# Turning x and the attention by VectorE blocks and DMAs instead of by TensorE

## The chip, the cores and the metric

The kernel runs on one core of a Trainium2 chip. The metric is the device time of one execution in microseconds (us). A core has five engines that run side by side, each with its own queue in program order: TensorE (PE; its weight loads are listed as PEld), VectorE (DVE), ScalarE (ACT), GpSimd (POOL) and SyncE (SP, here used to issue DMAs). Sixteen DMA engines move the data. The data is 32-bit floats throughout.

## The reference

The input x has 128 samples of 128 nodes by 512 features; `adj` is a 128x128 matrix. Four layers follow each other, each with a residual and a layer norm. Cut to what is computed:

```python
x = norm(x + (adj @ x) @ W0 + bias)                              # layer 0

q, k, v = x @ Wq.T, x @ Wk.T, x @ Wv.T                           # layer 1
rel = adj.T * (q @ k.T)                                          # per sample, 128x128
rel = rel / l2norm(rel, rows)
x = norm(x + rel @ v)

h = x @ W2                                                       # layer 2
e = leaky_relu(s1[:, None] + s2[None, :]) * adj                  # s1 = h @ a1, s2 = h @ a2
att = softmax(e, axis=-1)
x = norm(x + elu(att @ h + beta * h))

a = adj @ x                                                      # layer 3
x = norm(x + max over features of relu(...))                     # x gets one value per row
```

Layer 2 is computed as `elu((att + beta I) @ x @ W2)`: beta is added on the diagonal of the attention, so one product serves both terms.

## The kernel before

The samples are worked off in 32 groups of four (`G = 4`, `NG = 32`). Every piece of work has a place in a table, given in steps; a group takes 28 steps, and the pieces of all groups are emitted in order of place, so that the layers of neighbouring groups interleave on each engine. The four large products (`y`, `m`, `v`, `z`) use a Strassen-like scheme of seven steps of eight matmuls, whose sums (`x_sums`, `z_sums`, ...) GpSimd computes.

TensorE multiplies along the partitions, so several operands have to be turned (transposed) first. Layer 1 turns x on TensorE, sixteen 128x128 turns a group, and ScalarE copies the result out of PSUM:

```python
def turn(b):                                    # layer 1, sample b of the group
    if b == 0:
        s["xT"] = work.tile([P, K, G * P], FP, tag="aT_x", name=f"xT_{g}")
    p = bank(f"p_xT_{g}_{b}")
    for k in range(K):
        pe.transpose(p[:, k * P : (k + 1) * P], x1[g][:, b, k * P : (k + 1) * P], ident)
    act.copy(s["xT"][:, :, b * P : (b + 1) * P], p.rearrange("p (k n) -> p k n", k=K))
```

The relation matrix of layer 1 is turned in another way: VectorE turns square blocks of 32, and sixteen DMAs put the blocks where they belong. Two samples are interleaved, so that a run is 256 bytes:

```python
def turn_rel():
    # ... tiles relB and relT
    for b in range(G):
        dve.transpose(
            s["relB"][:, b // 2].rearrange("p q (u j) -> p q u j", j=2)[:, :, :, b % 2],
            s["rel"][:, b, :].rearrange("p (q u) -> p q u", q=Q),
        )

def move_rel(a):                                # a = 0..3
    n = P // Q                                  # 32
    for q in range(Q):                          # Q = 4
        sync.dma_start(
            s["relT"][q * n : (q + 1) * n, :, 2 * a * n : 2 * (a + 1) * n],
            s["relB"][a * n : (a + 1) * n, :, q, :],
        )
```

Layer 2 makes the attention `e` (names as in the profile: `nm` the negative maximum, `rs` the reciprocal sum), turns it on TensorE, four turns a group, and VectorE adds beta on the way out of PSUM. `gather` then forms `zT` sample by sample:

```python
def weighted():
    pool.tensor_tensor(s["e"], s["e"], adj_b, ALU.mult)
# ... greatest (DVE), exps (ACT)
def divide(i):
    # ... dve.reciprocal(rs, ...)
    engine = pool if n == G else dve
    engine.tensor_tensor(e, e, rs[:, :, None].to_broadcast([P, n, P]), ALU.mult)

def turn_att(i):
    # ...
        pe.transpose(s["p"][:, b * P : (b + 1) * P], s["e"][:, b, :], ident)

def with_beta(i):
    # ...
    dve.tensor_tensor(s["eT"][...], s["p"]..., beta_b[...], ALU.add)

def gather(b):
    # ...
        pe.matmul(p[:, k * P : (k + 1) * P], x2[g][:, b, k * P : (k + 1) * P],
                  s["eT"][:, b, :], start=True, stop=True)
    act.copy(s["zT"][:, :, b * P : (b + 1) * P], ...)
```

In the profile `p_xT` are the turns of x, `p_eT` those of the attention, `p_z` the gather, `p_o` the product with relT, `p_a` layer 3, `p_y` the aggregation of layer 0, `p_rel` the scores, `p_s` the spread of s2, and `r_y`, `r_m`, `r_v`, `r_z` the steps of the four large products. The three tiles tT (the M product), v and c (the z product) rotate through three buffers of one tag, `nat`; the weights wq, wk, wv lie in them at the start.

Of the kernel before, what the change touches and what calls it, by code (L numbers as in the profile page):

```python
# [8 lines left out]
FP = mybir.dt.float32  # L9
AF = mybir.ActivationFunctionType  # L10
ALU = mybir.AluOpType
# [18 lines left out]
def kernel(  # L30
# [33 lines left out]
    pe, dve, act, pool = (InOrder(tc, e) for e in (nc.tensor, nc.vector, nc.scalar, nc.gpsimd))  # L64
    sync = InOrder(tc, nc.sync)
    B, N, D = x.shape
    P = 128
    assert N == P and D % P == 0
    K = D // P
    Q = P // 32  # L70
    H = D // 2
    G = 4
# [5 lines left out]
    work = ctx.enter_context(tc.tile_pool(name="work", bufs=1))  # L78
# [3 lines left out]
    def bank(name):  # L82
        return psum.tile([P, D], FP, tag="ps", name=name)
# [8 lines left out]
    x1, x2, x3 = {}, {}, {}  # L92
# [12 lines left out]
    bias_sb = const.tile([P, D], FP)  # L105
    nc.scalar.dma_start(bias_sb, on_all(bias0, D))

    wq_sb = work.tile([P, K, D], FP, tag="nat", name="wq_sb", bufs=3)
    nc.sync.dma_start(wq_sb, wq.rearrange("(k p) f -> p k f", p=P))
    wk_sb = work.tile([P, K, D], FP, tag="nat", name="wk_sb", bufs=3)  # L110
    nc.sync.dma_start(wk_sb, wk.rearrange("(k p) f -> p k f", p=P))
    wv_sb = work.tile([P, K, D], FP, tag="nat", name="wv_sb", bufs=3)
    nc.sync.dma_start(wv_sb, wv.rearrange("(k p) f -> p k f", p=P))

    w2_sb = const.tile([P, K, D], FP)
# [25 lines left out]
    beta_b = beta_i[:, None, :].to_broadcast([P, G, P])  # L141
# [78 lines left out]
    def emit(at, f, *args):  # L220
        pieces.append((at, lambda: f(*args)))

    def each(at, f):
        for b in range(len(at)):
            emit(at[b], f, b)

    def row(at, step, n=G):
        return [at + i * step for i in range(n)]
# [2 lines left out]
    TABLE = dict(  # L231
        load=[-20], y=row(0.5, 1), bias=row(1.3, 1), y_sums=row(5.2, 0.5), y_w=row(7, 1, 7),
        stats0=row(14.4, 0.4), norm0=[16.2], apply0=row(16.8, 0.33),
        turn=row(21.4, 1), x_sums=row(25.3, 0.5), m=row(28, 1, 7), scores=row(36.5, 1),
        masked=[39.95], squares=[40.4], turn_rel=[40.3],
        move_rel=row(41.2, 0.1), inverse=[42.5], v=row(42, 1, 7), attend=row(50.6, 1),
        residual=row(51.0, 1), dots=row(54.2, 1.1), norm1=[55.2], scale=[58.8],
        apply1=row(65.4, 0.33),
        spread=[61.6], leaky=[62.0], weighted=[63.4], greatest=[64.3], exps=[64.4],
        divide=[65.8], turn_att=[68.6], with_beta=[69.0], gather=row(71.5, 1),  # L240
        z_sums=row(75.3, 0.5), z_w=row(77, 1, 7), exp=[87.5, 88.5, 90.4, 92.0],
        elu=[87.8, 89.4, 92.8, 93.8], norm2=[95.0], apply2=row(95.7, 0.33),
        widen=[98.7, 100.0, 103.6, 104.6], top=[99.1, 100.4, 104.0, 105.0],
        stats3=[99.8, 101.1, 104.7, 105.7], norm3=[106.2], apply3=row(107, 0.33), store=[108.5],
    )

    FIRST = {1: dict(y=row(-9.5, 0.3), bias=row(-9.2, 0.3))}

    LAST = {
        NG - 3: dict(  # L250
            exp=[0.8, 1.5, 2.2, 11.0], elu=[9.7, 12.3, 14.6, 17.2], norm2=[19.5],
# [2 lines left out]
        ),  # L254
        NG - 2: dict(
            scale=[5.6], apply1=row(24.3, 0.8), spread=[6.9], leaky=[7.4], weighted=[9.0],
            greatest=[10.5], exps=[11.2], divide=[13.6], turn_att=[18.3], with_beta=[18.9],
            gather=row(36.7, 0.9), z_sums=row(39.95, 1.3),
            z_w=[40.0, 41.8, 43.5, 45.2, 47.0, 49.4, 51.1], exp=[51.5, 52.2, 56.2, 58.6],
            elu=row(56.9, 2.3), norm2=[66.1], apply2=row(67.7, 0.8), widen=row(73.0, 0.86),  # L260
# [4 lines left out]
            m=[0.0, 1.73, 3.46, 5.2, 7.4, 9.1, 10.8], scores=row(12.7, 0.9), masked=[16.4],  # L265
# [3 lines left out]
            greatest=[52.4], exps=row(53.2, 0.6), divide=row(53.9, 0.6),  # L269
            turn_att=row(54.4, 0.6), with_beta=row(54.9, 0.6), gather=[55.2, 56.1, 60.5, 65.0],  # L270
            z_w=[57.0, 61.5, 66.0, 69.5], exp=[60.6, 65.0, 69.6, 73.2],
# [10 lines left out]
    def times(g):  # L282
        t = {key: [28.0 * g + v for v in at] for key, at in TABLE.items()}
        t.update({key: [28.0 * g + v for v in at] for key, at in FIRST.get(g, {}).items()})
        t.update({key: [LAST_M + v / SLOT for v in at] for key, at in LAST.get(g, {}).items()})
# [7 lines left out]
    def left_factors(at, s, aT, tag, name, keep):  # L293

        def blk(nh, kh):
            return s[aT][:, 2 * kh : 2 * kh + 2, 2 * P * nh : 2 * P * (nh + 1)]

        def first():  # L300
            sums = work.tile([P, 3 + keep, 2, 2 * P], FP, tag=tag, name=f"s_{name}")
            s1, s2, s4 = (sums[:, i] for i in range(3))
            s3 = sums[:, 3] if keep else blk(1, 0)
            s["f"] = {1: blk(0, 0), 2: blk(0, 1), 3: s4, 4: blk(1, 1), 5: s1, 6: s2, 7: s3}
            pool.tensor_tensor(s1, blk(1, 0), blk(1, 1), ALU.add)

        emit(at[0], first)
        emit(at[1], lambda: pool.tensor_tensor(s["f"][6], s["f"][5], blk(0, 0), ALU.subtract))
        emit(at[2], lambda: pool.tensor_tensor(s["f"][7], blk(0, 0), blk(1, 0), ALU.subtract))
        emit(at[3], lambda: pool.tensor_tensor(s["f"][3], blk(0, 1), s["f"][6], ALU.subtract))  # L310
# [129 lines left out]
    def layer1(g, t):  # L440
        s = {}

        def turn(b):
            if b == 0:
                s["xT"] = work.tile([P, K, G * P], FP, tag="aT_x", name=f"xT_{g}")
            p = bank(f"p_xT_{g}_{b}")
            for k in range(K):
                pe.transpose(
                    p[:, k * P : (k + 1) * P], x1[g][:, b, k * P : (k + 1) * P], ident
                )  # L450
            act.copy(
                s["xT"][:, :, b * P : (b + 1) * P], p.rearrange("p (k n) -> p k n", k=K)
            )

        def begin_middle():
            s["tT"] = work.tile([P, K, G * P], FP, tag="nat", name=f"tT_{g}", bufs=3)

        def middle_block(nh, ch):
            return s["tT"][:, 2 * ch : 2 * ch + 2, 2 * P * nh : 2 * P * (nh + 1)]
# [48 lines left out]
            pool.tensor_tensor(s["rn"], s["n2"], mhalf, ALU.pow)  # L508

        def begin_values():  # L510
            s["v"] = work.tile([P, G, D], FP, tag="nat", name=f"v_{g}", bufs=3)

        def attend(b):
            s["o", b] = bank(f"p_o1_{g}_{b}")
# [37 lines left out]
        def scale_dots():  # L552
# [11 lines left out]
            )  # L564
            s12[g] = s["d"]

        each(t["turn"], turn)
        left_factors(t["x_sums"], s, "xT", "s_x", f"x_{g}", 1)
        product(t["m"], f"m_{g}", by_columns, s, "m", middle_block, True, begin_middle)
        each(t["scores"], scores)  # L570
        emit(t["masked"][0], masked)
        emit(t["squares"][0], squares)
        emit(t["turn_rel"][0], turn_rel)
        each(t["move_rel"], move_rel)
        emit(t["inverse"][0], inverse)
        product(t["v"], f"v_{g}", by_rows, s, "v", rows_of(lambda: s["v"]), True, begin_values)
        each(t["attend"], attend)
        each(t["residual"], residual)
# [9 lines left out]
    def layer2(g, t):  # L588
        s = {}
# [40 lines left out]
        def divide(i):  # L630
            rs = small.tile([P, n], FP, tag=f"rs{n}", name=f"rs_{g}_{i}")
            dve.reciprocal(rs, s["sums"][:, i * n : i * n + n])
            e = s["e"][:, i * n : i * n + n, :]
            engine = pool if n == G else dve
            engine.tensor_tensor(e, e, rs[:, :, None].to_broadcast([P, n, P]), ALU.mult)

        def turn_att(i):
            if i == 0:
                s["p"] = bank(f"p_eT_{g}")
            for b in range(i * n, i * n + n):  # L640
                pe.transpose(s["p"][:, b * P : (b + 1) * P], s["e"][:, b, :], ident)
# [25 lines left out]
            )  # L667

        def begin():
            s["c"] = work.tile([P, G, D], FP, tag="nat", name=f"c_{g}", bufs=3)  # L670
            for b in range(G):
                s["c", b] = s["c"][:, b, :]

# [26 lines left out]
        n = G // len(t["exps"])  # L700
# [3 lines left out]
        emit(t["greatest"][0], greatest)  # L704
        each(t["exps"], exps)
        each(t["divide"], divide)
        each(t["turn_att"], turn_att)
        each(t["with_beta"], with_beta)
        each(t["gather"], gather)
        if g < NG - 1:  # L710
            left_factors(t["z_sums"], s, "zT", "s_yz", f"z_{g}", 0)
            product(t["z_w"], f"z_{g}", by_rows, s, "2", rows_of(lambda: s["c"]), True, begin)
        else:
            each(t["z_w"], direct)
# [39 lines left out]
    for g in range(NG):  # L754
        for layer in (layer0, layer1, layer2, layer3):
            layer(g, times(g))
# [31 lines left out]
```

## Time and profile before

| what | value |
|---|---|
| time, median of 3 executions | 2263.68 us (2263.55 to 2263.74) |
| span of the profiled execution | 2260.3 us |
| turns of x on PE (`p_xT`) | 512 |
| turns of the attention on PE (`p_eT`) | 128 |
| ACT copies of the turned x, mean | 586 ns, 128 of them |
| DVE add of beta (`eT<-p_eT,beta_i`), mean | 630 ns, 35 of them |
| DVE block turn of 128x128 (`relB<-rel`), mean | 283 ns, 128 of them |
| relT DMAs (SP queue) | 512 of 16 KB |

In the profile a group of instructions is given as engine, operation, tiles (out<-in), shapes, count, busy time and mean duration. Timeline lines give the start, the duration, the engine and the instruction, and in square brackets how long the engine was idle before it and what ended that. Durations of neighbouring instructions overlap in part[...]; the distance between two starts is what an instruction costs its engine. "to landing" of a DMA is the time from its issue until its semaphore says that the data is there.

### The profile page before, as it was taken

Reading aid. Unit: us, or ns where it says so; the run is one execution under the profiler, and the core shown is the slowest. Engines: PE = TensorE matmul, PEld = TensorE weight load, DVE = VectorE, ACT = ScalarE, POOL = GpSimd, SP = SyncE. Lnnn points to the kernel's source line nnn. Section 1 sums busy time; section 2 is a strip of 40 time slices with the busy share of each in tenths; the row PEclk is TensorE's granted clock in tenths of the full one; section 3 lists DMA queues with packets and bytes.
Section 4 is the critical chain, followed back from the end, with each engine's and each line's share of the span. In section 5 each row is a group of like instructions: output and inputs, shape, how many; then the busy total and the mean of one; then the engine's idle time right before and its main releaser. Section 6 shows DMA issues by size and latency. Waiting matters only on the chain.

```text
span 2260.3 us, 31788 instructions
## 1 busy us (share of the span) xinstructions
PE 2221.2 (98%) x11553; PEld 1884.2 (83%) x11553; DVE 1599.1 (71%) x3414; ACT 1043.4 (46%) x2056; POOL 924.4 (41%) x743
## 2 busy tenths in 40 slices
PE   7999999999999999999999999999999999999996
PEld 5888888888888888888888888888888888888873
DVE  4657776667766767766767766677767677667678
ACT  2235444454444454444454444544444544444545
POOL 3434444334444334444334443444443344443322
PEclk9999999999999999999999999999999999999998
DMA  4000111100111100111101111001111001110001
GB/s 164 24 24 9 40 39 42 43 24 25 43 38 43 42 24 25 41 40 43 43 12 37 39 42 43 24 24 43 38 43 43 25 24 42 39 43 24 15 15 56
DMA packets 79853, 83.67 MB, mean 37 GB/s; under 512 B 43985, under 2 KB 44113, under 8 KB 79697
## 3 DMA queue, kind: packets, MB, share of 16 engines
q1 hardware_dynamic: 78496, 79.28, 10.5%
q10 hardware_dynamic: 1200, 2.36, 0.3%
q8 instruction: 92, 1.51, 0.3%
q14 instruction: 65, 0.52, 0.1%
HBM read 39.65 MB, written 33.55 MB: 32 GB/s over the span
## 4 chain that ended last, share of the span: by engine, by line
PE 93%; DVE 4%; POOL 1%; ACT 1%; issue 1%; DMA 0%; ACTq 0%; DVEq 0%; POOLq 0%
PE r_y L26 17%; PE r_v L26 16%; PE r_m L26 16%; PE r_z L26 16%; PE p_rel L26 5%; PE p_z L26 5%; PE p_o L26 5%; PE p_y L26 5%; PE p_a L26 5%; PE p_xT L26 2%; DVE x L26 1%; DVE st L26 1%; PE p_eT L26 1%; PE p_m L26 1%; PE p_s L26 1%
## 5 line engine op out<-in xcount | busy, mean ns | idle before, releaser
L26 ACT ACTIVATE x<-x,nmean,rstd 128x512 f32<-128x512 f32 x512 | 389.0, 808 | 127.4 <-DVE nmean L26 127.2
L26 DVE BATCH_NORM_STATS2 st<-x 128x6 f32<-128x512 f32 x512 | 352.2, 688 | 74.8 <-ACT x L26 66.0
L26 POOL TENSOR_TENSOR rstd<-ve,mhalf 128x4 f32<-128x4 f32 (+1 forms) x134 | 144.5, 1078 | 360.0 <-DVE ve L26 356.0
L26 POOL TENSOR_TENSOR x<-x,bias_sb 128x512 f32<-128x512 f32 x128 | 173.9, 1361 | 146.5 <-PE p_y L26 146.5
L26 DVE SCALAR_TENSOR_TENSOR scr<-x,wa 128x512 f32<-128x512 f32 x256 | 214.4, 888 | 0.0
L26 ACT ACTIVATE x<-x,top 128x512 f32<-128x512 f32 x128 | 92.4, 722 | 225.3 <-DVE top L26 225.1
L26 DVE TENSOR_TENSOR v<-r_v,v 128x512 f32<-128x512 f32 x96 | 65.8, 685 | 178.5 <-PE r_v L26 175.5
L26 POOL TENSOR_TENSOR s_x<-xT 128x512 f32<-128x512 f32 x64 | 82.1, 1282 | 223.1 <-ACT xT L26 223.1
L26 DVE TENSOR_TENSOR x<-r_y,x 128x512 f32<-128x512 f32 x224 | 151.7, 678 | 30.2 <-PE r_y L26 29.8
L26 ACT COPY yT<-p_y 128x512 f32<-128x512 f32 x128 | 75.2, 587 | 205.7 <-PE p_y L26 205.7
L26 DVE SCALAR_TENSOR_TENSOR x<-p_o,rn,x 128x512 f32<-128x512 f32 x128 | 95.9, 749 | 100.0 <-PE p_o L26 97.1
L26 DVE SCALAR_TENSOR_TENSOR x<-m,x 128x512 f32<-128x512 f32 x128 | 114.8, 897 | 61.4 <-ACT m L26 51.4
L26 ACT COPY c<-r_z 128x512 f32<-128x512 f32 x124 | 72.7, 586 | 176.0 <-DVE scr L26 174.9
L26 PEld LDWEIGHTS p_y<-adjT,x 128*128 128x128 f32 x1024 | 135.0, 194 | 13.0 <-ACT adjT L26 5.1
L26 PE MATMUL p_y<-adjT,x 128*128 128x128 f32 x1024 | 135.8, 277 | 6.3 <-ACT adjT L26 4.8
L26 PEld LDWEIGHTS p_z<-eT,x 128*128 128x128 f32 x1024 | 133.9, 192 | 8.4 <-DVE x L26 1.2
L26 PEld LDWEIGHTS p_rel<-xT,tT 128*128 128x128 f32 x1024 | 134.1, 191 | 7.4 <-DVE tT L26 0.8
L26 PE MATMUL p_rel<-xT,tT 128*128 128x128 f32 x1024 | 134.9, 275 | 0.6 <-DVE tT L26 0.6
L26 PE MATMUL p_z<-eT,x 128*128 128x128 f32 x1024 | 134.8, 275 | 0.4 <-DVE x L26 0.4
L26 PE MATMUL p_a<-x,adjT 128*128 128x512 f32 x256 | 131.2, 597 | 3.6 <-ACT x L26 1.9
L26 ACT COPY tT<-r_m 128x512 f32<-128x512 f32 x128 | 75.7, 591 | 123.7 <-PE r_m L26 123.7
L26 POOL TENSOR_TENSOR s_z<-zT 128x512 f32<-128x512 f32 x31 | 39.2, 1263 | 225.7 <-ACT zT L26 225.7
(118 smaller groups left out, 5119.0 us busy)
## 6 DMA issues: line engine op xcount, KB each, us to landing
out_dram<-x SPq DMA_DIRECT2D x128, 256.0 KB, 2.0
x<-in_x_dram SPq DMA_DIRECT2D x31, 1024.0 KB, 5.3
relT<-relB SPq DMA_DIRECT2D x512, 16.0 KB, 1.8
w_sb<-in_L_gnn_weight_dram ACTq DMA_DIRECT2D x1, 1024.0 KB, 5.8
x<-in_x_dram SPq DMA_DIRECT2D x4, 256.0 KB, 7.7
wq_sb<-in_L_gnn_Wq_dram SPq DMA_DIRECT2D x1, 1024.0 KB, 12.2
wk_sb<-in_L_gnn_Wk_dram SPq DMA_DIRECT2D x1, 1024.0 KB, 14.9
w_sb<-in_L_gnn_W_dram ACTq DMA_DIRECT2D x1, 1024.0 KB, 10.1
```

The source lines that it names most:

```text
L26: return lambda *args, **kw: self.tc.keep_in_program_order(op(*args, **kw))
```

## The change

From group 2 on, x is turned as the relation matrix already was: VectorE turns blocks of 32, and sixteen DMAs move the blocks. From group 0 to the last but one, so is the attention. Here samples aren't interleaved, and a run is 128 bytes. The beta is then added on GpSimd, before the turn, right after the division. The purpose is to take twenty turns a group off TensorE, and four copies off ScalarE. Room for the new tiles (xB, eB) comes from the buffers: tT and v now share one buffer (`tv`), and c has one of its own. The table moves: the block turns and moves of x stand at steps 18.4 and 20.5 (the turns on TensorE began at 21.4), the attention's at 67.5 and 68.0 (before 68.6), `gather` goes from 71.5 to 72.4 and `z_sums` from 75.3 to 76.3.

```diff
-    wq_sb = work.tile([P, K, D], FP, tag="nat", name="wq_sb", bufs=3)
+    wq_sb = work.tile([P, K, D], FP, tag="tv", name="wq_sb")
     # likewise wk_sb: tag "c", wv_sb: tag "xB"
     TABLE = dict(
-        turn=row(21.4, 1), x_sums=row(25.3, 0.5), ...
+        turn=row(21.4, 1), turn_blocks=row(18.4, 0.6),
+        move=row(20.5, 0.1), x_sums=row(25.3, 0.5), ...
-        divide=[65.8], turn_att=[68.6], with_beta=[69.0], gather=row(71.5, 1),
-        z_sums=row(75.3, 0.5), ...
+        divide=[65.8], turn_att=[67.5], move_att=row(68.0, 0.1), gather=row(72.4, 1),
+        z_sums=row(76.3, 0.5), ...
     # FIRST and LAST: places of the first and of the last groups
     # layer 1
+        def turn_blocks(b):
+            if b == 0:
+                s["xB"] = work.tile([P, Q, K, G, P // Q], FP, tag="xB", name=f"xB_{g}")
+                s["xT"] = work.tile([P, K, G * P], FP, tag="aT_x", name=f"xT_{g}")
+            dve.transpose(
+                s["xB"][:, :, :, b, :].rearrange("p q k u -> p k q u"),
+                x1[g][:, b, :].rearrange("p (k q u) -> p k q u", k=K, q=Q),
+            )
+        def move(a):
+            n = P // Q
+            for q in range(Q):
+                sync.dma_start(
+                    s["xT"][q * n : (q + 1) * n].rearrange("p k (b n) -> p (k b) n", b=G)[
+                        :, :, a * n : (a + 1) * n
+                    ],
+                    s["xB"][a * n : (a + 1) * n, q].rearrange("p k b n -> p (k b) n"),
+                )
-            s["tT"] = work.tile([P, K, G * P], FP, tag="nat", name=f"tT_{g}", bufs=3)
+            s["tT"] = work.tile([P, K, G * P], FP, tag="tv", name=f"tT_{g}")
     # likewise v: tag "tv"; c: tag "c"
-        each(t["turn"], turn)
+        if g < 2:
+            each(t["turn"], turn)
+        else:
+            each(t["turn_blocks"], turn_blocks)
+            each(t["move"], move)
     # layer 2
             engine.tensor_tensor(e, e, rs[:, :, None].to_broadcast([P, n, P]), ALU.mult)
+            if n == G:
+                pool.tensor_tensor(e, e, beta_b, ALU.add)
+        def turn_blocks():
+            s["eB"] = work.tile([P, Q, G, P // Q], FP, tag="eB", name=f"eB_{g}")
+            s["eT"] = work.tile([P, G, P], FP, tag="eT", name=f"eT_{g}")
+            for b in range(G):
+                dve.transpose(
+                    s["eB"][:, :, b, :], s["e"][:, b, :].rearrange("p (q u) -> p q u", q=Q)
+                )
+        def move(a):
+            m = P // Q
+            for q in range(Q):
+                sync.dma_start(
+                    s["eT"][q * m : (q + 1) * m, :, a * m : (a + 1) * m],
+                    s["eB"][a * m : (a + 1) * m, q],
+                )
-        each(t["turn_att"], turn_att)
-        each(t["with_beta"], with_beta)
+        if n < G:
+            each(t["turn_att"], turn_att)
+            each(t["with_beta"], with_beta)
+        else:
+            emit(t["turn_att"][0], turn_blocks)
+            each(t["move_att"], move)
```

In the last group (`n < G`) the attention is still turned on TensorE.

More of the change, by code (lines that the diff above doesn't have):

```diff
@@ L106 @@
     nc.scalar.dma_start(bias_sb, on_all(bias0, D))
-    wq_sb = work.tile([P, K, D], FP, tag="nat", name="wq_sb", bufs=3)
+    wq_sb = work.tile([P, K, D], FP, tag="tv", name="wq_sb")
     nc.sync.dma_start(wq_sb, wq.rearrange("(k p) f -> p k f", p=P))
-    wk_sb = work.tile([P, K, D], FP, tag="nat", name="wk_sb", bufs=3)
+    wk_sb = work.tile([P, K, D], FP, tag="c", name="wk_sb")
     nc.sync.dma_start(wk_sb, wk.rearrange("(k p) f -> p k f", p=P))
-    wv_sb = work.tile([P, K, D], FP, tag="nat", name="wv_sb", bufs=3)
+    wv_sb = work.tile([P, K, D], FP, tag="xB", name="wv_sb")
     nc.sync.dma_start(wv_sb, wv.rearrange("(k p) f -> p k f", p=P))
@@ L233 @@
         stats0=row(14.4, 0.4), norm0=[16.2], apply0=row(16.8, 0.33),
-        turn=row(21.4, 1), x_sums=row(25.3, 0.5), m=row(28, 1, 7), scores=row(36.5, 1),
+        turn=row(21.4, 1), turn_blocks=row(18.4, 0.6),
+        move=row(20.5, 0.1), x_sums=row(25.3, 0.5), m=row(28, 1, 7), scores=row(36.5, 1),
         masked=[39.95], squares=[40.4], turn_rel=[40.3],
@@ L239 @@
         spread=[61.6], leaky=[62.0], weighted=[63.4], greatest=[64.3], exps=[64.4],
-        divide=[65.8], turn_att=[68.6], with_beta=[69.0], gather=row(71.5, 1),
-        z_sums=row(75.3, 0.5), z_w=row(77, 1, 7), exp=[87.5, 88.5, 90.4, 92.0],
+        divide=[65.8], turn_att=[67.5], move_att=row(68.0, 0.1), gather=row(72.4, 1),
+        z_sums=row(76.3, 0.5), z_w=row(77, 1, 7), exp=[87.5, 88.5, 90.4, 92.0],
         elu=[87.8, 89.4, 92.8, 93.8], norm2=[95.0], apply2=row(95.7, 0.33),
@@ L245 @@
     )
-    FIRST = {1: dict(y=row(-9.5, 0.3), bias=row(-9.2, 0.3))}
+    FIRST = {0: dict(turn=row(20.4, 0.3)), 1: dict(y=row(-9.5, 0.3), bias=row(-9.2, 0.3))}
     LAST = {
@@ L256 @@
             scale=[5.6], apply1=row(24.3, 0.8), spread=[6.9], leaky=[7.4], weighted=[9.0],
-            greatest=[10.5], exps=[11.2], divide=[13.6], turn_att=[18.3], with_beta=[18.9],
+            greatest=[10.5], exps=[11.2], divide=[13.6], turn_att=[17.6], move_att=row(18.8, 0.1),
             gather=row(36.7, 0.9), z_sums=row(39.95, 1.3),
@@ L510, in begin_values @@
         def begin_values():
-            s["v"] = work.tile([P, G, D], FP, tag="nat", name=f"v_{g}", bufs=3)
+            s["v"] = work.tile([P, G, D], FP, tag="tv", name=f"v_{g}")
         def attend(b):
@@ L669, in begin @@
         def begin():
-            s["c"] = work.tile([P, G, D], FP, tag="nat", name=f"c_{g}", bufs=3)
+            s["c"] = work.tile([P, G, D], FP, tag="c", name=f"c_{g}")
             for b in range(G):
```

## The prediction

> **What bounds the kernel now.** I read the page from the top: busy shares, then the chain that ended last, then one steady group by windows, then the timeline of that group. The batch is worked off in 32 groups of four; in the steady part one group follows another every 68.59 us.
>
> ```profile
> PE 2221.2 (98%) x11553; PEld 1884.2 (83%) x11553; DVE 1599.1 (71%) x3414; ACT 1043.4 (46%) x2056; POOL 924.4 (41%) x743
> PE 93%; DVE 4%; POOL 1%; ACT 1%; issue 1%; DMA 0%; ACTq 0%; DVEq 0%; POOLq 0%
> 1000.00:1068.59 68.59, 68.59 (x362) 58.72 (x361) 49.14 (x105) 32.46 (x65) 28.86 (x23) 1.00 0.11 35
> ```
>
> The first line gives busy time per engine, the second the shares of the chain. The third is one whole group: length, then busy us of PE, PE's weight loads, DVE, ACT, POOL, then clock and DMA share. TensorE (PE) is busy in all 68.59 us at full clock. So TensorE sets the time: an instruction taken off it shortens a group by its full slot, provided that everything TensorE waits for still comes in time. DVE has 19 us to spare, ACT 36, POOL 40.
>
> The slot of a turn is read from starts in the timeline, since durations (0.60) overlap:
>
> ```profile
> 1018.88 1.89 PE L26 MATMUL r_y<-w_sb,s_y 128*128 128x256 f32 x8
> 1020.60 0.60 PE L26 MATMUL p_eT<-ident,e 128*128 128x128 f32 x4
> 1021.04 1.89 PE L26 MATMUL r_y<-t,yT 128*128 128x256 f32 x8
> 1022.77 1.89 PE L26 MATMUL r_v<-wvT,xT 128*128 128x256 f32 x8
> 1024.50 1.02 PE L26 MATMUL p_a<-x,adjT 128*128 128x512 f32 x2
> 1025.36 1.89 PE L26 MATMUL r_v<-wvT,xT 128*128 128x256 f32 x8
> 1027.08 1.05 PE L26 MATMUL p_z<-eT,x 128*128 128x128 f32 x8
> 1027.97 1.02 PE L26 MATMUL p_a<-x,adjT 128*128 128x512 f32 x2
> 1028.83 1.89 PE L26 MATMUL r_v<-t_v,s_x 128*128 128x256 f32 x8
> ...
> 1043.59 0.60 PE L26 MATMUL p_xT<-ident,x 128*128 128x128 f32 x4
> 1044.03 1.89 PE L26 MATMUL r_z<-w_sb,zT 128*128 128x256 f32 x8
> ```
>
> Four turns take 1021.04 - 1020.60 = 0.44 us of TensorE, and the four of one x the same. An r step takes 1.73 us, a p_a 0.86.
>
> The rest of the attention's chain, and the transfer that already works as the new ones will:
>
> ```profile
> 1009.02 1.27 POOL L26 TENSOR_TENSOR e<-e,adj_sb 128x512 f32<-128x512 f32 x1 [0.63 <-DVE e L26]
> 1016.85 0.15 DVE L26 RECIPROCAL rs<-sums 128x4 f32<-128x4 f32 x1
> 1017.14 1.04 POOL L26 TENSOR_TENSOR e<-e,rs 128x512 f32<-128x512 f32 x1 [6.85 <-DVE rs L26]
> 1020.74 0.90 DVE L26 STREAM_TRANSPOSE relB<-rel 128x128 f32<-128x128 f32 x4
> L26 SPq DMA_DIRECT2D relT<-relB x16: 591/595/597, 1021.7 to 1031.3; - x16
> relT<-relB SPq DMA_DIRECT2D x512, 16.0 KB, 1.8
> 1026.00:1028.00 2.00, 2.00 (x15) 1.87 (x14) 1.90 (x6) 0.72 (x1) 0.00 (x0) 1.00 0.11 25
> ```
>
> The relation matrix is already turned by DVE blocks and 16 DMAs. Their issues start at 1021.7 and 1031.3, so one every 9.6 / 15 = 0.64 us, and each lands 1.8 us after its issue. While they run, the DMA engines are 11% busy: the sequencer that issues, not the engines, paces them.
>
> [...] here the blocks are turned first, so the DMAs move runs of 128 bytes. [...] 0.11 x 16 engines x 2.00 us = 3.5 us in 2 us, for 2 / 0.64 = 3.1 DMAs of 64 data and 16 semaphore packets, so some 14 ns a packet. No run yet shows 128 bytes. [...]
>
> **The change part by part.**
>
> Removed from TensorE: 30 groups (2 to 31) lose 16 turns of x, 31 groups (0 to 30) lose 4 of the attention. That is 30 x 4 x 0.44 + 31 x 0.44 = 66.4 us, or 5 x 0.44 = 2.20 us of each steady group. If all of it came through: 68.59 - 2.20 = 66.39 us a group, 2197 us in all.
>
> Removed from ACT: four copies of 0.586 us a group, not on the path. On DVE: the beta add on the turned attention, 0.63 us, goes. DVE gains four block turns of 128x512 (estimate: four 128x128 turns take 0.90 us as a row, so about 0.8 each, 3.2) and four of 128x128 (0.90): net +3.5 us, to about 53 of 66. POOL gains the beta add, 1.27 us as the equal multiplication by adj: 30 of 66. Both fit in sum. A shared buffer for M and V loses nothing I can see: V's last reader (p_o) stands before M's first write.
>
> Added on the DMA queue: 16 DMAs a group for x (64 KB each, 512 runs) and 16 for the attention (16 KB, 128 runs). Engines: 10,240 packets x at most 15 ns / 16 = 10 us a group, harmless. Issue: 32 x 0.64 = 20.5 us beside relT's 10.2, the stores and a load (5): 36 of 66, so the queue fits too. What matters is latency: a row of 16 needs 15 x 0.64 + 1.8 = 11.4 us from first issue to last landing.
>
> Is x turned in time? The built program puts these DMAs on the queue in the order attention, rel, x. X's transfers wait for the last DVE block turn (after p_a's third maximum) and for the old xT's last reader, r_v at 1039.28. They can start about 1043 (with the wait below) and land at about 1055. Their first reader, r_m, starts one period before 1061.8; it moves to about 1062. Some 7 us of slack: the path is hidden, and stays so up to about 1.1 us an issue.
>
> Is the attention turned in time? In clock times of the group above: rs ends at 1017.0; POOL divides until 1018.2 and adds beta until 1019.5; DVE turns from 1019.6 to 1020.5; DMAs issue from 1020.6; the last issue is at 1030.2, the last landing at 1032.0. The first p_z needs all 16, since each writes a part of all four samples. When does TensorE get there? The changed order moves p_z behind one more p_a and one more r_v. From 1020.60: r_y 1.73, r_v 1.73, p_a 0.86, r_v 1.73, p_a 0.86, r_v 1.73, so 1029.2. TensorE then waits 2.8 us.
>
> The sum of a group: 68.59 - 2.20 + 2.8 = 69.2. Nothing upstream of rs gets earlier by the change: DVE works from the M product (tT at 1003.05, where it waited 1.15 us for TensorE) to rs nearly without a gap, in unchanged order, and no turn leaves TensorE between the two. So the wait recurs in every group. Groups 0 to 29 have it (the 31st has its own schedule, with gather long after the transfer): 2263.7 - 66.4 + 30 x 2.8 = 2281 us.
>
> **The rivals.**
>
> A: everything hidden, 2197 us. For it: idle engines and an idle queue, and the author's table leaves 4.4 of its steps (28 steps make a group, so 2.4 us each, 10.6 us) between transfer and gather. Against: a row takes 11.4 us, and POOL's two operations and DVE's turn stand in front. It needs issues at 0.45 us or less; a store of 2 KB rows issues in 0.33 us by the queue's own rows, so the 0.595 of relT is not a law for every shape.
>
> B (my choice): the attention's latency replaces the turns, and gives back somewhat more than they cost, 2281 us.
>
> C: runs of 128 bytes issue or move slower with their number. If an x DMA with 512 runs took 1.3 us to issue, x would land about 3 us after r_m wants it: 2281 + 30 x 3 = 2370. If the attention's took 0.8, its wait would grow by 2.4 us a group, to 2353. Against: a load of 512 rows of 2 KB issues in 0.39 us by the same rows, less than relT's with 64, so number alone doesn't slow issue.
>
> D: DVE becomes the bound. Against: 53 of 66 us. But it is dense around rs, and waiting there for POOL's beta shifts rel and the normalisation by 1.4 us; TensorE's p_a has about that much slack. I count nothing.
>
> E: the waits cost clock. [...]
>
> **Range and chances.** The centre is B, 2281, with the wait known to about 1 us (30 us in all). Below lie mixtures with A (an issue of 0.55 us saves 1.4 us a group: 2240), above C and E. I take 2215 to 2360. Faster by over 2% means under 2218, a wait under 0.7 us: 0.18. Slower by over 2% means over 2309, a wait over 3.7 us: 0.26. Between: 0.56.
>
> **What would show it.** Right: a steady group of about 69.2 us with TensorE busy about 66.4; the wait of p_z on the attention's transfer in every group, 2 to 3.5 us; issues every 0.64 us for both new transfers; no wait of r_m on xT; PEclk still 9s. Wrong: no wait at p_z (then issue is faster than relT's), a wait at r_m (then runs matter), or DVE as releaser before p_a or p_o.

## The result, and the profile after

| | before | after |
|---|---|---|
| time, median | 2263.61 us | 2365.88 us |
| ratio, 95% interval | | 1.0451 [1.0433, 1.0469] |
| one steady group, mean | 68.59 us | 71.98 us |

The change made the kernel 4.5% slower. The prediction was 2281 us, with a range to 2360.

The page of the kernel after, first the busy line and then the shares of the chain that ended last:

```profile
PE 2212.1 (93%) x10949; PEld 1851.5 (78%) x10949; DVE 1802.2 (76%) x3627; ACT 983.7 (42%) x1936; POOL 1019.4 (43%) x774
...
PE 46%; DVE 27%; SPq 12%; POOL 7%; issue 5%; DMA 3%; ACT 1%; DVEq 0%; ACTq 0%; POOLq 0%
```

TensorE's share of the chain fell from 93% to 46%. The rest now runs through DVE, the DMA queue that issues (SPq) and POOL. That is the mark of a loop: the chain leaves TensorE and comes back to it, group after group.

Where TensorE waits, from the view of waits of the kernel after (total us, times, longest):

```profile
PE p_z L26 <- DMA eT<-eB: 66.5, 30, 3.9
PE r_y L26 <- DVE x L26: 44.0, 43, 1.7
```

The first was predicted. The second was not. Both are seen in one group in the timeline of the kernel after (start, duration, engine, instruction; in brackets the idle time before it and what ended it):

```profile
1208.42 0.14 DVE L26 RECIPROCAL rs<-sums 128x4 f32<-128x4 f32 x1
1208.71 1.04 POOL L26 TENSOR_TENSOR e<-e,rs 128x512 f32<-128x512 f32 x1 [6.85 <-DVE rs L26]
1209.82 1.26 POOL L26 TENSOR_TENSOR e<-e,beta_i 128x512 f32<-128x512 f32 x1
1211.05 1.02 POOL L26 TENSOR_TENSOR rstd<-ve,mhalf 128x4 f32<-128x4 f32 x1
1211.12 0.89 DVE L26 STREAM_TRANSPOSE eB<-e 128x128 f32<-128x128 f32 x4 [1.35 <-POOL e L26]
1212.04 10.29 SPq L26 DMA_DIRECT2D eT<-eB  x16
1212.10 0.16 DVE L26 SCALAR_TENSOR_TENSOR nmean<-mv,rstd 128x4 f32<-128x4 f32 x1
1212.17 0.69 DVE L26 TENSOR_TENSOR x<-r_y,x 128x512 f32<-128x512 f32 x1
...
1209.95 1.89 PE L26 MATMUL r_y<-w_sb,s_y 128*128 128x256 f32 x8
1212.92 1.99 PE L26 MATMUL r_y<-t,yT 128*128 128x256 f32 x8 [1.08 <-DVE x L26]
1214.75 1.89 PE L26 MATMUL r_v<-wvT,xT 128*128 128x256 f32 x8
1216.48 1.02 PE L26 MATMUL p_a<-x,adjT 128*128 128x512 f32 x2
1217.34 1.89 PE L26 MATMUL r_v<-wvT,xT 128*128 128x256 f32 x8
1219.06 1.02 PE L26 MATMUL p_a<-x,adjT 128*128 128x512 f32 x2
1219.92 1.89 PE L26 MATMUL r_v<-t_v,s_x 128*128 128x256 f32 x8
1223.69 1.13 PE L26 MATMUL p_z<-eT,x 128*128 128x128 f32 x8 [1.88 <-DMA eT<-eB]
```

Read it from the top. From rs, the way to p_z is divide, beta, blocks, sixteen DMAs and a landing: 15.27 us here, 15.63 in the mean. On DVE, eB waits for POOL's beta; nmean, which needs POOL's rstd from behind beta, and the next x<-r_y stand after eB. TensorE's last r_y step needs that x<-r_y, so TensorE is stopped there first and at p_z again.

The same group in the view of windows, cut at p_z, p_o, rs and the next p_z (length, then busy us of PE, its weight loads, DVE, ACT, POOL, then clock, DMA share and GB/s):

```profile
1152.19:1169.59 17.40, 17.40 (x85) 14.83 (x86) 7.95 (x17) 8.68 (x14) 5.25 (x5) 0.90 0.17 32
1169.59:1208.43 38.84, 38.84 (x203) 33.49 (x202) 34.47 (x63) 15.57 (x31) 21.19 (x15) 1.00 0.27 74
1208.43:1223.70 15.27, 12.31 (x57) 9.58 (x55) 12.59 (x35) 6.22 (x16) 5.29 (x5) 1.00 0.12 19
1152.19:1223.70 71.51, 68.56 (x341) 57.89 (x341) 55.01 (x113) 30.47 (x60) 31.73 (x24) 0.98 0.22 52
```

In this group TensorE is idle only in the third row, and its clock is down only in the first: 0.90. The clock's loss shows in the timeline of the kernel after. The first three lines follow a wait of 1.89 us, the last two a wait of 1.88 us (at 1223.69 above):

```profile
1152.18 1.13 PE L26 MATMUL p_z<-eT,x 128*128 128x128 f32 x8 [1.89 <-DMA eT<-eB]
1153.15 3.20 PE L26 MATMUL r_v<-wvT,s_x 128*128 128x256 f32 x8
1156.14 1.47 PE L26 MATMUL p_z<-eT,x 128*128 128x128 f32 x8
...
1224.65 1.89 PE L26 MATMUL r_v<-wvT,s_x 128*128 128x256 f32 x8
1226.38 1.05 PE L26 MATMUL p_z<-eT,x 128*128 128x128 f32 x8
```

The r_v step takes 3.20 us in place of 1.89. The clock records give full speed after the second wait, and half speed for 3.4 us after the first. The way from p_z to p_o is then 17.4 us and not 15.72.

The mean of groups 2 to 27, split by TensorE's starts: 66.39 us of work, 2.36 waiting at p_z, 1.54 at the last r_y step, 1.12 lost at half clock (half of the 2.23 us a group that the clock records give), 0.57 in short waits and slow steps elsewhere: 71.98.

### The profile page after: what moved, and what is told of

It reads as the page before. It is cut to its first block, busy times and chain, and to the rows that moved or that the text cites. A ratio compares the mean times of both kernels' runs of the same rounds, so it can differ in the third digit from the quotient of the medians.

```text
span 2367.5 us, 32301 instructions
## 1 busy us (share of the span) xinstructions
PE 2212.1 (93%) x10949; PEld 1851.5 (78%) x10949; DVE 1802.2 (76%) x3627; ACT 983.7 (42%) x1936; POOL 1019.4 (43%) x774
## 3 DMA queue, kind: packets, MB, share of 16 engines
q10 hardware_dynamic: 1200, 2.36, 0.3%
HBM read 39.65 MB, written 33.55 MB: 31 GB/s over the span
## 4 chain that ended last, share of the span: by engine, by line
PE 46%; DVE 27%; SPq 12%; POOL 7%; issue 5%; DMA 3%; ACT 1%; DVEq 0%; ACTq 0%; POOLq 0%
PE r_z L26 13%; SPq L26 12%; DVE x L26 11%; PE r_v L26 10%; PE r_m L26 6%; PE p_z L26 6%; DVE scr L26 5%; POOL e L26 5%; PE p_o L26 4%; DVE st L26 4%; DMA eT<-eB 2%; PE p_y L26 2%; PE p_a L26 2%; DVE tT L26 2%; DVE e L26 2%
## 5 line engine op out<-in xcount | busy, mean ns | idle before, releaser
L26 DVE SCALAR_TENSOR_TENSOR scr<-x,wa 128x512 f32<-128x512 f32 x256 | 284.0, 1161 | 0.0
L26 POOL TENSOR_TENSOR x<-x,bias_sb 128x512 f32<-128x512 f32 x128 | 194.3, 1527 | 78.5 <-PE p_y L26 77.9
L26 PE MATMUL p_z<-eT,x 128*128 128x128 f32 x1024 | 150.6, 295 | 69.0 <-DMA eT<-eB 66.5
L26 PEld LDWEIGHTS p_z<-eT,x 128*128 128x128 f32 x1024 | 144.5, 208 | 87.5 <-issue 51.3
L26 POOL TENSOR_TENSOR s_x<-xT 128x512 f32<-128x512 f32 x64 | 96.2, 1502 | 252.7 <-DMA xT<-xB 225.6
L26 PE MATMUL r_y<-t,yT 128*128 128x256 f32 x512 | 124.1, 385 | 40.2 <-DVE x L26 40.2
L26 DVE STREAM_TRANSPOSE xB<-x 128x512 f32<-128x512 f32 x120 | 81.2, 696 | 95.3 <-ACT x L26 51.9
L26 ACT COPY zT<-p_z 128x512 f32<-128x512 f32 x128 | 75.0, 586 | 178.0 <-PE p_z L26 172.3
L26 PE MATMUL r_v<-wvT,s_x 128*128 128x256 f32 x512 | 141.5, 427 | 0.9 <-ACT v L26 0.9
L26 PEld LDWEIGHTS r_y<-t,yT 128*128 128x128 f32 x512 | 92.4, 190 | 61.9 <-DVE x L26 51.9
```

The lines of the kernel that those rows point to most:

```text
L26: return lambda *args, **kw: self.tc.keep_in_program_order(op(*args, **kw))
```

## The theories

**The loop** (mine, after the result). Three legs follow each other and close. From p_z to p_o TensorE works alone. From p_o to rs TensorE goes on to the M product, and from its tT VectorE works to rs (elu, residuals, statistics); beside TensorE's part VectorE has residuals and dots to do, and if these take longer, they set the leg. From rs back to p_z runs the attention's way. If the sum of the legs is above TensorE's 66.4 us, the sum is the group.

**The sum**: TensorE's work, plus each wait as a cost of its own that stays what it is. The prediction's total has this form, though its wait was worked out along the legs (see "Why the prediction was wrong"). The rivals inside it: the r_y wait is a second cost; the shared buffers cost something; the DMAs of x do.

The experiments below, as legs between starts (us, means of groups 4 to 27; the group is taken one p_z later, so that a row's legs can differ from it by some hundredths):

| kernel | p_z to p_o | p_o to rs | rs to p_z | group | clock | time, us |
|---|---|---|---|---|---|---|
| before | 19.11 | 39.26 | 10.22 | 68.59 | 0.996 | 2263.6 |
| after | 16.87 | 39.65 | 15.63 | 72.08 | 0.981 | 2365.9 |
| x alone | 18.24 | 39.88 | 9.56 | 67.68 | 0.996 | 2236.5 |
| attention alone | 17.02 | 39.26 | 15.57 | 71.83 | 0.990 | 2363.8 |
| eight matmuls before p_z | 15.65 | 39.71 | 16.70 | 72.06 | 0.995 | 2368.7 |
| four DMAs on ScalarE | 15.69 | 39.57 | 13.48 | 68.74 | 0.994 | 2271.9 |
| four matmuls before p_z | 15.73 | 39.87 | 15.62 | 71.21 | 0.994 | 2345.0 |
| diagonal beta | 15.95 | 39.59 | 12.10 | 67.65 | 0.995 | 2239.0 |
| x alone, early | 18.24 | 38.36 | 10.22 | 66.81 | 0.998 | 2210.9 |
| r_y freed | 17.62 | 39.46 | 15.42 | 72.50 | 0.968 | 2388.4 |
| after, x early | 17.03 | 38.48 | 15.62 | 71.06 | 0.979 | 2338.0 |
| the three together | 15.70 | 38.57 | 12.30 | 66.56 | 0.996 | 2210.2 |

In the kernel before and in "x alone, early" TensorE does not stop in the steady part: its work sets the sum, and the third leg has slack in it. Where the attention is turned on TensorE, p_z stands one p_a and one r_v earlier, which makes the first leg some 2.5 us longer (18.24 against 15.72).

## The experiments

**x alone.** The attention goes back to TensorE, with its places in the table.

```diff
-        if n < G:
+        if True:   # attention: turn_att and with_beta as before, beta not on POOL
```

> Only x is turned by blocks and DMAs; the attention is turned on TensorE with beta added by VectorE, at the places of the kernel before. Theory 'loop' (a group of the changed kernel, 72.0 us, is set by the loop p_z to p_o on TensorE 15.7, p_o to rs on VectorE 40.2, rs to p_z over POOL, VectorE and 16 DMAs 15.7, plus clock lost in the wait): without the transfers the loop is some 11 us shorter and TensorE bounds again: 68.59 - 1.76 = 66.8 us a group, 2263.6 - 30 x 1.76 = 2211 us, at most a small wait of p_eT (VectorE reaches rs up to 1 us later), so 2211 to 2235. Rival 'x late' (the transfers of x and the POOL sums behind them, which now run beside the dots of VectorE, cause the loss): stays at 2300 or more.

Measured: 2236.49 us, ratio 0.9886 [0.9872, 0.9901]. The half of the change that concerns x gains, by 1.1%, and its DMAs are not the harm. But 67.68 us a group is 0.85 above the 66.83 that is left without x's turns (68.59 - 4 x 0.44). That remainder is taken up below.

**The attention alone.** x stays on TensorE.

```diff
-        if g < 2:
+        if True:   # x: turn, as before
```

> Only the attention is turned by blocks and DMAs, x on TensorE. Theory 'loop': p_z to p_o takes 15.6 + 0.88 for two turns of x = 16.5, p_o to rs 39.2 to 40.2, rs to p_z 15.7, so 71.4 to 72.4 us a group, plus up to 1.3 of lost clock: 2348 to 2390, about the time of the whole change although TensorE has 53 us more work. Theory 'sum' (TensorE's work plus waits of fixed length): 2366 + 30 x 1.76 = 2419. Rival 'x late': near the kernel before less 0.44 us a group, 2250 to 2270.

Measured: 2363.81 us, ratio 1.0444 [1.0427, 1.0462], as slow as the whole change. The attention's way alone brings the loss, and a wait of fixed length is excluded (2419 expected, 2364 measured). TensorE does 1.76 us more work a group than in the kernel after, in nearly the same time (71.83 and 72.08). That two such kernels meet is chance, and no sign that TensorE's work has ceased to count: x's turns lie on the first two legs, 0.88 us ahead of p_o (16.60 us in place of 15.72 where the clock is whole) and 0.90 us between p_o and r_m (12.97 in place of 12.07). The whole change saves both, and loses 1.3 us in the second leg and 0.7 us more of clock.

**Matmuls into the wait.** To see what the clock costs, source matmuls of no use keep TensorE busy ahead of p_z.

```diff
+                if 0 < g < NG - 2:
+                    idle = bank(f"p_idle_{g}")
+                    for i in range(8):      # the second run: 4
+                        pe.matmul(idle[:, :H], w2_sb[:, i % K, :P],
+                                  w2_sb[:, i % K, H:], start=True, stop=True)
```

> The changed kernel with eight idle matmuls (1.73 us of TensorE, results unused) ahead of the first p_z of groups 1 to 29. If half-clock stretches come from TensorE standing idle in the wait: the matmuls lie inside the wait of p_z (2.4 us on average), the clock stays at full, the 1.5 us of slow steps a group go, and the time falls by 25 to 45 us to 2320 to 2340 although work is added. If the slow steps have another cause: unchanged at 2366 or up to 29 x 1.7 = 50 us longer.

Measured: 2368.65 us, ratio 1.0468 [1.0452, 1.0484]. Inconclusive by itself, and by my sizing: a source matmul is two in the trace, so eight took 3.45 us. The first leg fell to 15.65, so the clock was whole, but p_z was pushed 1.07 us back. With four:

> The changed kernel with four extra matmuls (1.73 us by the size that the run with eight showed) ahead of TensorE's wait for eT. Loop theory, with the clock as a part of it: the half-clock stretches go away or nearly so, the fill ends before eT lands, so nothing is pushed later; the group falls from 72.0 to 70.6-71.2 us, the whole to 2320-2345 us, granted clock above 0.99. If the clock loss is not part of the loop: unchanged at 2360-2372 us.

Measured: 2344.99 us, ratio 1.0364 [1.0348, 1.0379], at the upper edge. The third leg is unmoved (15.62), the first falls from 16.87 to 15.73. The lost clock is therefore worth 1.1 us of the first leg. The group falls by 0.9, because the second leg is 0.2 us longer here; 71.2 is the sum of the legs at whole clock.

**Four DMAs on another queue.**

```diff
-                sync.dma_start(
+                (act if a == 3 and g < NG - 2 else sync).dma_start(
```

> The changed kernel with the last 4 of the 16 attention transfers issued by ScalarE, beside the 12 of SyncE. If the issue rate of one queue (0.64 us each) sets the landing: the last landing comes 4 x 0.64 = 2.6 us earlier, the loop falls to about 69.1 us and most of the lost clock returns (up to 1.3): 68.6 to 69.4 us a group, 2260 to 2290 us. If the DMA engines or the small runs set it: unchanged, 2360 to 2370.

Measured: 2271.9 us, ratio 1.0042 [1.0027, 1.0057]. Two microseconds off the third leg, and the group falls by 3.3, since the clock's loss goes too. The wait at p_z is 0.13 us a group, while the r_y wait is still 1.57. Taking four issues out of a row of sixteen brings back 94 of the 102 us that the change lost.

**Beta on the diagonal alone.** Beta stands only on the diagonal, so twelve of sixteen blocks need none. POOL adds no beta; the four diagonal blocks go to eT by four small VectorE adds.

```diff
-                pool.tensor_tensor(e, e, beta_b, ALU.add)
+                if q == a:
+                    continue                  # no DMA for a diagonal block
+        def diagonal():                       # after the twelve DMAs
+            for q in range(Q):
+                sl = slice(q * m, (q + 1) * m)
+                dve.tensor_tensor(s["eT"][sl, :, sl], s["eB"][sl, q],
+                    beta_i[sl, None, sl].to_broadcast([m, G, m]), ALU.add)
```

> The full change, but beta is added on the diagonal blocks alone by four small VectorE adds that write eT, POOL adds no beta, and 12 DMAs instead of 16 carry the rest. Loop theory: eB 1.3 us earlier and 4 issues of 0.64 us fewer, so rs to p_z falls from 15.6 to 11-12.5 us, the loop from 71.6 to about 67.5; waits of p_z below 0.5 us, wait of the last r_y step down to 0.5 us or less because eB no longer stands ahead of x<-r_y waiting for POOL; group 66.5-67.8 us, whole 2200-2240 us. Fixed-wait theory (the sum of the prediction: 66.4 plus a wait that shortens by 3.9 us): about the same time, but then the p_z wait would be nil at once and the r_y wait unchanged, 2235-2260 us.

Measured: 2238.99 us, ratio 0.9891 [0.9874, 0.9907]. The third leg is 12.10 us, the wait at p_z 0.04, the r_y wait about 0.4; the loop's figures, though the time lies at the upper end and the sum theory's 2235 would do as well. What is left on DVE at the r_y step is short: nmean waits 0.23 us for POOL's rstd.

**Buffers.** The kernel before with the tags of the changed one (`tv`, `c`, `xB`).

```diff
-            s["v"] = work.tile([P, G, D], FP, tag="nat", name=f"v_{g}", bufs=3)
+            s["v"] = work.tile([P, G, D], FP, tag="tv", name=f"v_{g}")
     # likewise tT: "tv"; c: "c"
```

> The kernel before with the shared buffer of M and V and the smaller pools alone; TensorE turns stay. Loop theory: buffers play no part, 2260-2267 us. If sharing the buffer adds a wait of its own (V's write waiting for M's last reader), 2275 us or more.

Measured: 2262.83 us, ratio 1.0001 [0.9992, 1.001], every steady group 68.59. Sharing the buffer costs nothing in the kernel before.

**x alone, earlier.** In "x alone" the dots last 1176 ns in the mean, before 888. POOL's s_x, which waits for the DMAs of x, now runs beside them. This run moves x's blocks and DMAs ahead, for which xT needs two buffers.

```diff
-        turn_blocks=row(18.4, 0.6), move=row(20.5, 0.1),
+        turn_blocks=row(18.4, 0.3), move=row(19.6, 0.1),
-                s["xT"] = work.tile(..., tag="aT_x", name=f"xT_{g}")
+                s["xT"] = work.tile(..., tag="aT_x", name=f"xT_{g}", bufs=2)
     # room for it: rel with one buffer
```

> x alone by blocks and DMAs, with two buffers of xT and its blocks and DMAs about 6 us earlier in the group, so that POOL's s_x runs before VectorE's dots. If the dots' slowing beside s_x is what keeps x alone above its 66.4 us a group: dots back to a length near 7.2 us, group 66.6-67.1 us, whole 2208-2222 us. If the residual has another cause: 2230-2240 us, as x alone was.

Measured: 2210.88 us, ratio 0.9769 [0.9755, 0.9784]; every steady group 66.81. The page's group of the dots, first of the kernel after and then of this one (busy us, mean ns):

```profile
L26 DVE SCALAR_TENSOR_TENSOR scr<-x,wa 128x512 f32<-128x512 f32 x256 | 284.0, 1161 | 0.0
```

```profile
L26 DVE SCALAR_TENSOR_TENSOR scr<-x,wa 128x512 f32<-128x512 f32 x256 | 204.4, 850 | 0.0
```

The timeline of the kernel after shows how a mean of 1161 arises:

```profile
1180.69 1.71 POOL L26 TENSOR_TENSOR s_x<-xT 128x512 f32<-128x512 f32 x1
1182.36 1.72 POOL L26 TENSOR_TENSOR s_x<-xT,s_x 128x512 f32<-128x512 f32 x1
...
1181.21 1.74 DVE L26 SCALAR_TENSOR_TENSOR scr<-x,wa 128x512 f32<-128x512 f32 x1
...
1184.63 0.68 DVE L26 SCALAR_TENSOR_TENSOR scr<-x,wa 128x512 f32<-128x512 f32 x1
```

A dot takes 0.68 us, or 1.74 when a 128x512 addition runs on POOL; the addition grows too, from 1.27 to 1.7. In this run the four s_x end before the first dot starts.

**r_y freed.** The x<-r_y that TensorE waits for is put ahead of eB and nmean on VectorE. It does not need either.

```diff
-        turn_att=[67.5], ...  apply2=row(95.7, 0.33),
+        turn_att=[67.9], ...  apply2=row(96.05, 0.33),
```

> The changed kernel with VectorE's order moved in one place: the x<-r_y that TensorE's last r_y step waits for stands ahead of the blocks eB and of the nmean that waits for POOL's rstd, not behind them. The r_y wait should go from 1.5 us a group to 0.3 or less, eB starts no later. Theory of the sum (each wait is a cost of its own): 71.98 - 1.3, so 70.3-70.7 us a group, 2320-2335 us. Loop theory (rs and what follows it set when p_z may start; the r_y wait lies inside that time): p_z's wait takes over what the r_y wait gives up and rises to about 3.8 us, group 71.7-72.5 us, 2355-2385 us, granted clock the same or lower.

Measured: 2388.41 us, ratio 1.055 [1.0532, 1.0568], just above the loop's range. This run tells the two theories apart most clearly: a wait of 1.5 us is removed, and the kernel gets slower. Its timeline, the same steps as shown above:

```profile
1213.57 1.89 PE L26 MATMUL r_y<-w_sb,s_y 128*128 128x256 f32 x8
1215.30 1.89 PE L26 MATMUL r_y<-t,yT 128*128 128x256 f32 x8
...
1227.25 1.88 PE L26 MATMUL p_z<-eT,x 128*128 128x128 f32 x8 [3.16 <-DMA eT<-eB]
1228.92 1.49 PE L26 MATMUL r_v<-wvT,s_x 128*128 128x256 f32 x3
```

The r_y step starts with no idle time, TensorE arrives earlier at p_z and waits there for longer: 3.80 us in the mean, against 2.36 and 1.54 before. The longer waits of this run also cost more clock: the first leg is 1.90 us above 15.72, against 1.15. So 72.43 us a group (groups 2 to 27) against 71.98.

**After, x early.** The changed kernel with the earlier x; nothing between rs and p_z is touched. The tile that the dots write and nobody reads is given one buffer for room.

```diff
     # x as in "x alone, earlier", in the changed kernel
-            scr = work.tile([P, D], FP, tag="scr", ..., bufs=2)
+            scr = work.tile([P, D], FP, tag="scr", ..., bufs=1)
```

> The changed kernel with x's blocks and DMAs about 6 us earlier and two buffers of xT, as in the run of x alone, attention as changed. Loop theory: the dots no longer run beside s_x, rs comes 1.2-1.5 us earlier after p_o, so the loop and the group fall by that much although nothing between rs and p_z is touched: 70.4-70.9 us a group, 2318-2340 us. Fixed-wait theory (rs follows TensorE, its path to p_z is what it was): 2358-2372 us, unchanged.

Measured: 2337.97 us, ratio 1.0329 [1.0313, 1.0344], within the loop's range. rs comes 1.17 us earlier after p_o, the third leg stays at 15.62, the wait at p_z at 2.36, and the group falls by 1.02. VectorE waits for TensorE at tT again, 0.91 us in the mean, as it did before the change. The group was expected at 70.4 to 70.9 and is 71.06; the lost clock did not shrink with it.

**The three together**: diagonal beta, early x, r_y freed.

> Beta on the diagonal blocks alone, 12 DMAs, x's moves early with two buffers of xT, and x<-r_y ahead of eB: the three together. Loop theory: 15.7 from p_z to p_o, 38.3 to rs, 11.9 to p_z, 65.9 us, below TensorE's own 66.4, so TensorE's work alone is left: 66.4-66.8 us a group, no wait of p_z or r_y, 2195-2212 us. If VectorE's longer list (it carries the blocks of x and of the attention and the diagonal) now sets the pace itself: 67.0 us or more, 2218 us or more.

Measured: 2210.2 us, ratio 0.9767 [0.9752, 0.9781]. One group of each of the two fastest kernels in the view of windows, "x alone, earlier" first:

```profile
1008.00:1074.81 66.81, 66.81 (x346) 57.18 (x346) 51.66 (x109) 30.34 (x61) 28.91 (x23) 1.00 0.21 52
```

```profile
1008.00:1074.37 66.37, 66.37 (x341) 56.66 (x341) 55.31 (x115) 30.19 (x60) 29.45 (x24) 1.00 0.23 55
```

TensorE is busy throughout in both. In the second kernel 12 of 26 steady groups are at 66.37 to 66.40 us, the prediction's 66.39; others are up to 1.2 us longer. The legs expected at 65.9 measured 66.57, as long as TensorE's work, so the loop has no slack; that this makes the longer groups is likely and not shown. What it gains over "x alone, earlier" in the steady part, 0.25 us a group, it loses in the first and last groups; I did not follow that further. The two can't be told apart, and the simpler one leaves the attention alone.

## Why the prediction was wrong

**What held.** 66.39 us of TensorE's work: shown by the last run. The x path hidden from TensorE: no wait of r_m on xT in the kernel after. Rival C, that 128-byte runs are slow: sixteen DMAs of 512 runs took 10.7 us to issue, sixteen of 128 runs 10.5, landing after 2.3 and 1.8 us. The wait at p_z was 2.36 us, within the 2 to 3.5 that were named, but by luck: TensorE stops for 3.90 us a group, of which 1.54 fall at the r_y step. PEclk "still 9s" holds in the page's line only because that is a mean over 60 us; the windows show 0.90.

**The step that failed.** Written as legs, the prediction is the same loop: 15.72 from p_z to p_o; 38.36 from p_o to rs (39.26 less the 0.90 of x's turns that leave ahead of r_m); 15.15 from the start of rs to the last landing (1032.0 - 1016.85). Their sum is its 69.2. The path was right; two of its terms were too small, and the clock's loss was left out. The step that failed worst is "DVE works from the M product (tT at 1003.05, where it waited 1.15 us for TensorE) to rs nearly without a gap, in unchanged order", with "Both fit in sum" behind it.

- The second leg is 39.65 us, not 38.36: 1.3 us. Before the change VectorE is ahead of TensorE at tT, and waits there. In the kernel after it has just done its dots, in many groups too late. The lines of tT, before, after, and after with x early:

```profile
1003.05 0.69 DVE L26 TENSOR_TENSOR tT<-r_m,tT 128x512 f32<-128x512 f32 x1 [1.15 <-PE r_m L26]
```

```profile
1194.12 0.69 DVE L26 TENSOR_TENSOR tT<-r_m,tT 128x512 f32<-128x512 f32 x1 [0.18 <-PE r_m L26]
```

```profile
1180.09 0.69 DVE L26 TENSOR_TENSOR tT<-r_m,tT 128x512 f32<-128x512 f32 x1 [1.15 <-PE r_m L26]
```

In the means of groups 4 to 27 the dots take 9.4 us a group after the change and 7.0 before. The wait at tT is 0.09 us in place of 1.15, and in 12 of 24 groups it is below 0.05. From tT to rs VectorE takes 14.45 us in place of 13.81; in the group shown the residual x<-c after tT takes 1.18 us where 0.69 did before (0.70 again with x early); that this too comes of POOL's shifted additions is likely and not shown. With the attention alone, where x stays on TensorE, wait and way are as before (1.15 and 13.82); with x alone, early, too (1.15 and 13.81, a leg of 38.36). Busy time was counted, and not what two engines do to each other. The trace of the kernel after shows it: no dot without a 128x512 operation of POOL beside it takes more than 0.69 us (48 of them), and the median of the 101 wholly beside such operations (s_x, and the additions of the bias) is 1.74; the statistics, with one input, stay at 0.69 (their group's mean is 688 ns in both kernels). That early x makes the dots short again and takes the time off the leg is shown by two runs (1.52 us in x alone, 1.17 in the whole change); why a dot and an operation of POOL slow each other is not shown.
- The clock: the first leg is 16.87 us in place of 15.72, so 1.15 us. This was rival E, left out of the centre; the trace of the kernel before, with no wait in its steady part, did not show what a wait costs. Waits of 1.89 us and more were followed by half clock, though not all of them (last part); the run with four matmuls gives 1.14 us of it back.
- The third leg is 15.63, not 15.15: 0.5 us. From the start of rs to the first issue it was 3.62 us, and 3.75 in the prediction; from there to p_z 12.0 in place of 11.4, half of it because an issue took 0.66 us and not 0.64, and 0.23 us from the last landing to the start of p_z.

69.2 + 1.3 + 1.15 + 0.5 = 72.15, the sum of the measured legs. By the mean of groups 2 to 27, 71.98, a group is 2.8 us above the prediction; over 30 groups that is 84 us, and the result lies 85 above.

**Rival D.** I saw that VectorE would wait for POOL's beta and counted nothing, naming p_a as the reader with slack. The wait came at another reader, the last r_y step, 1.54 us a group. To count nothing was right all the same: the freed run shows that this wait lies inside the loop, and costs nothing while p_z waits.

**Rival A** (all hidden, 2197 us) was close for a changed form of the kernel: 12 issues and no beta on POOL, with x early and r_y freed, bring the steady group to 66.56.

## What to carry to other kernels

When work leaves the engine that sets the time, look for the next loop, not the next wait: mark one event on each engine that work passes through, add the legs round one period, and compare the sum with the engine's own work; a wait inside the loop can be removed without any gain. A chain that was hidden at a distance of 10 us can cost more at 15 than the removed work was worth (here 10.22 and 15.63 us, for 2.20 us of TensorE's work a group), so shorten it first (fewer transfers, or a second issuing queue) and move work afterwards. Sums of busy time do not show what two engines do to each other at the same time (here a dot took 1.74 us in place of 0.68): check what a moved transfer lets start, and beside what.

## What the hardware showed unexpectedly

- Waits of TensorE under 2 us already cost clock here, from 1.89 us on. In four kernels (after, attention alone, r_y freed, after with x early) I set each wait at p_z against the time from that p_z to p_o. None of 17 waits from 1.68 to 1.88 us was followed by a half-clock stretch, 48 of 73 from 1.89 to 3.26, and all 26 above. One stretch costs 1.7 us (17.40 - 15.72).
- What tells the 48 from the other 25 is nearly settled by the clock records. In each of the four traces the starts of the half-clock stretches lie whole multiples of 3.413 us apart (21, 22, 42, 43, ... of them; 21 starts in the kernel after), so in each trace they stand on one grid. Take of each wait only its longest piece within one cell of that grid: with pieces up to 1.88 us none of 39 waits was followed by half clock, from 1.89 to 1.97 us 11 of 14, above that all 63; 22 of the 25 have no piece of 1.89 us. So waits of the same length cost clock or not by where they fall: in the kernel after, p_o stood 17.40 us behind one p_z that had waited 1.90 us (572.82), and 15.72 behind another (1724.27). The two waits shown above, in the view of windows, cell by cell (length, PE's busy time, and the clock as the third number from the end):

```profile
1150.15:1153.57 3.42, 1.53 (x11) 1.38 (x11) 1.72 (x5) 0.94 (x2) 0.96 (x1) 1.00 0.15 28
1153.57:1156.98 3.41, 3.41 (x11) 2.87 (x10) 0.71 (x1) 2.26 (x4) 0.00 (x0) 0.50 0.11 24
```

```profile
1221.83:1225.25 3.42, 1.56 (x11) 1.54 (x12) 1.57 (x5) 1.12 (x2) 0.81 (x1) 1.00 0.12 23
1225.25:1228.66 3.41, 3.41 (x21) 3.10 (x21) 0.71 (x1) 3.27 (x6) 0.00 (x0) 1.00 0.13 29
```

TensorE is idle for 1.89 us in the first cell, and 1.86 in the third.

- The issue of a DMA cost the same for 512 runs of 128 bytes as for 128 (10.7 and 10.5 us for sixteen).
- A 128x512 block turn on VectorE took 696 ns, a 128x128 one 280 ns: the larger turn costs 2.5 times as much for four times the data. I had estimated 0.8 us.
